# Softmax denominators of a graph-attention kernel: piece sums added by TensorE, or by VectorE after a block transpose

## The chip, the cores and the metric

The kernel runs on one core of a Trainium2 chip. The metric is the device time of one launch in microseconds (us). A core has TensorE (PE; its weight loads are shown as PEld), VectorE (DVE), ScalarE (ACT), GpSimd (POOL) and SyncE (SP). They run on their own queues, each in order, and wait for each other through semaphores. SP, ACT and POOL also issue the transfers (DMA).

## What is computed

There are N = 3327 nodes with 512 features and an adjacency matrix. Four layers follow each other, and each ends in `x = layernorm(x + layer(x))`. Layers 0, 2 and 3 are graph attention with 8, 8 and 4 heads; layer 1 averages over the first 64 neighbours. The attention layers have this core (layer 0, per head; the others differ in the width of a head and in an ELU at the end):

```python
Wh = jnp.einsum('ni,hio->hno', h, W)
e = jax.nn.leaky_relu(f1[:, :, None] + f2[:, None, :], ALPHA)
masked = jnp.where(adj[None] > 0, e, NEG_INF)
attention = jax.nn.softmax(masked, axis=-1)
h_prime = jnp.einsum('hnm,hmo->hno', attention, Wh)
```

A softmax row is a weighted sum of Wh divided by a denominator, the sum of its weights. The kernel computes numerators and denominators separately and divides later. This case is about the last step of the denominators.

## The kernel before

**Stages.** The kernel goes through layer 0's projection, layer 0's attention, layer 1 in two phases (`sage`), layer 2's attention, layer 3's projection (`third`), layer 3's attention and a tail. Nodes are cut into NT = 26 tiles of 128. The target nodes are cut into two halves of IW = 1664. In an attention layer `attention` (L516) runs over the two halves and over four units s of 128 feature columns. A unit holds HS heads: two in layers 0 and 2, one in layer 3.

**A unit** (`unit`, L357) loops over the 26 source tiles j. For each head, VectorE makes t, 128 source nodes by 1664 target nodes (L398), and ScalarE makes y from it, a step between the pieces of the weight (L401). TensorE multiplies t into the numerators, four PSUM tiles po0 to po3 (L421). Every second j, `den` multiplies y and the mask by narrow matrices of bf16 pieces into two PSUM tiles pd0 and pd1 (L373): these are the denominators. A bf16 piece holds a third of an fp32 number's digits. Every head has two numbers of three pieces each, in eight columns of these matrices, and each column's sums lie on a partition of their own in pd. Partitions 0 to 63 of pd hold the first WA = 896 target nodes, and 64 to 127 the other WB = 768. In layers 0 and 2 both heads have a group of 32 partitions; in layer 3 even and odd j have one each. The t tiles have three buffers a head, so VectorE runs at most three j ahead of TensorE. The tiles vj, the operand of numerators, come by SP two j at a time into four buffers (L409).

**After the loop.** po is copied to ob in SBUF (L441, L443) or transposed there by VectorE in 32x32 blocks (L439, layer 3's first half). `transposed` (L446) turns ob tile by tile on TensorE through two rotating PSUM banks, copies to hb (L453, two buffers) and stores to hd in DRAM (L454). When the last unit of a half is through (in layer 3's second half after units 1, 2 and 3), the pieces are added. ScalarE (in layer 3 VectorE for half of it) copies pd to db (L474, L475). `sums` (L479) lets TensorE multiply 13 tiles of db by a narrow matrix of 2, -2 and 0 (c1, or c1w for one head), which adds the pieces and at the same time turns target nodes onto partitions. `reciprocals` (L491) does two operations per head on VectorE and a reciprocal, and leaves the factors in rec. `finish_steps` (L165) later multiplies the h tiles by rec (L180), adds the residual and normalises (L152 to L161).

**What sets the order.** TensorE's order is the order in which the program is written (`manual_schedule`). The other engines' instructions are ordered by a planner with costs of its own, by when it thinks each ready; `keep_in_program_order` pins an instruction behind everything that was written before it for its engine. What follows a unit is put into a list of jobs, and the next unit's loop takes one job after each j: `jobs[:2] + [sums, nothing, reciprocals] + jobs[2:]` puts the sums after j = 2, the reciprocals after j = 4 and the first ob transposes after j = 5. After the second half of a layer no unit follows. The jobs are then run through one after the other, and the next stage's first tiles come behind them.

Of the kernel before, what the change touches and what calls it, by code (L numbers as in the profile page):

```python
# [7 lines left out]
F32 = mybir.dt.float32  # L8
# [5 lines left out]
ALU = mybir.AluOpType  # L14
AX = mybir.AxisListType
# [3 lines left out]
P = 128  # L19
# [13 lines left out]
def kernel(  # L33
# [10 lines left out]
    nc = tc.nc  # L44
# [5 lines left out]
    NS = F // P  # L50
    HALF = NT // 2
    FW = F // 2
    assert F == 512 and NT % 2 == 0 and N < NP and NT < 32
    IW = HALF * P
    NA = (HALF + 1) // 2
    WA, WB = NA * P, IW - NA * P
# [3 lines left out]
    QUADS = [(s, min(4, HALF - s)) for s in range(0, HALF, 4)]  # L60
# [5 lines left out]
    dram = ctx.enter_context(tc.tile_pool(name="dram", bufs=1, space=DRAM))  # L66
    qp = ctx.enter_context(tc.tile_pool(name="q", bufs=2, space=PSUM))
# [30 lines left out]
    c1 = const.tile([P, 2, 16], F32, name="c1")  # L98
    c1w = const.tile([P, 2, 2, 4], F32, name="c1w")
# [5 lines left out]
    for e in range(2):  # L105
        nc.vector.tensor_tensor(c1w[:, :, e, :], c1[:, :, 8 * e:8 * e + 4], c1[:, :, 8 * e + 4:8 * e + 8],
                                op=ALU.add)
# [4 lines left out]
    rec = const.tile([P, NT, 8], F32, name="rec")  # L112
# [110 lines left out]
    class Layer:  # L223
# [133 lines left out]
        def unit(self, pools, half, s, background, aside, final=None, ending=None):  # L357
            H, D, HS = self.H, self.D, self.HS
            tp, yp, vp, rp, sp, po_p = pools
# [3 lines left out]
            po = [po_p.tile([P, 512], F32, name=f"po{c}") for c in range(4)]  # L363
# [3 lines left out]
            pd, seen = self.pd, self.seen  # L367
# [76 lines left out]
            t0 = half * HALF  # L444

            def transposed(s0, n):  # L446
                pt = qp.tile([P, 4, P], F32, name="pt", tag="q")
                for q in range(n):
                    nc.tensor.transpose(pt[:, q, :], ob[:, (s0 + q) * P:(s0 + q + 1) * P], ident)  # L449
                if final:  # L450
                    return final(s, s0, n, pt)
                hb = sp.tile([P, 4, P], F32, name="hb")
                nc.scalar.copy(hb[:, :n], pt[:, :n])  # L453
                nc.sync.dma_start(out=hd[(t0 + s0) * P:(t0 + s0 + n) * P, s * P:(s + 1) * P]  # L454
                                  .rearrange("(t p) f -> p t f", p=P), in_=hb[:, :n])

            nothing = lambda: None
            jobs = [nothing, nothing]
            if by_dma:
                for b in range(4):  # L460
                    nc.sync.dma_start(out=hd[i0:i0 + IW, s * P + 32 * b:s * P + 32 * b + 32]
                                      .rearrange("(q i) f -> i q f", i=32),
                                      in_=ob[32 * b:32 * b + 32, :].rearrange("p (q f) -> p q f", f=32))
# [3 lines left out]
            if s < NS - 1 and not (final and s > 0):  # L467
                return jobs

            db = sp.tile([P, WA], F32, name="db", bufs=1)  # L470
            if WB < WA:
                nc.gpsimd.memset(db[64:, WB:], 0.0)
            for c in range(2):
                nc.scalar.copy(db[:64, c * (WA // 2):(c + 1) * (WA // 2)], pd[c][:64, :WA // 2])  # L474
                (nc.scalar.copy if HS == 2 else nc.vector.tensor_copy)(  # L475
                    db[64:, c * (WB // 2):(c + 1) * (WB // 2)], pd[c][64:, :WB // 2])
            held = []

            def sums():  # L479

                pe = po[0][:, :2 * HALF * H].rearrange("p (q o h) -> p q o h", q=HALF, o=2) if final and s == NS - 1 else \
                    qp.tile([P, HALF, 2, H], F32, name="pe", tag="q")
                held.append(pe)
                for q in range(HALF):
                    e = int(q >= NA)
                    cc = c1[:, :, 8 * e:8 * e + 8] if HS == 2 else c1w[:, :, e, :]
                    nc.tensor.matmul(pe[:, q, :, :], db[:, (q - e * NA) * P:(q - e * NA + 1) * P], cc,  # L487
                                     start=True, stop=True)


            def reciprocals():  # L491
                pe = held[0]

                ss = slice(0, NS) if not final else slice(0, 2) if s == 1 else slice(s, s + 1)
                r_ = rec[:, t0:t0 + HALF, :H].rearrange("p t (s k) -> p t k s", k=HS)
                rc = self.rc[:, t0:t0 + HALF, :].rearrange("p t (s k) -> p t k s", k=HS)
                pv = pe.rearrange("p t o (k s) -> p t o k s", k=HS)
                for k in range(HS):
                    tc.keep_in_program_order(
                        nc.vector.tensor_tensor(r_[:, :, k, ss], pv[:, :, 0, k, ss], rc[:, :, k, ss], op=ALU.mult))  # L500
                    nc.vector.tensor_tensor(r_[:, :, k, ss], pv[:, :, 1, k, ss], r_[:, :, k, ss], op=ALU.add)
                hs = slice(ss.start * HS, ss.stop * HS)
                nc.vector.reciprocal(rec[:, t0:t0 + HALF, hs], rec[:, t0:t0 + HALF, hs])

            if final and s == NS - 1:

                take = []
                return [lambda: take.append(transposed(*QUADS[0])), lambda: take.append(transposed(*QUADS[1])),
                        sums, reciprocals] + [lambda q=q: take[q]() for q in range(2)] + \
                    [lambda q=q: transposed(*q)() for q in QUADS[2:]]  # L510
            return jobs[:2] + [sums, nothing, reciprocals] + jobs[2:]

# [568 lines left out]
```

## Time and profile before

| | |
|---|---|
| median of 3 runs | 3428.16 us (3425.46 to 3432.74) |
| profiled execution | 3434.45 us, span 3432.3 us, mean granted TensorE clock 0.982 |
| layer 0, attention | to 960 us |
| layer 1 and the projection of layer 2 | 960 to 1790 us |
| layer 2, attention | 1790 to 2576 us |
| layer 3, projection, attention and tail | 2576 to 3432 us |
| sums on TensorE (L487) | at 580, 963, 2194, 2577, 3064, 3239, 3325 and 3403 us; 26 records each |
| copies of pd to db | L474 ACT 64x448: 0.52 us; L475 ACT 64x384: 0.47 us, DVE 64x384: 0.56 us |

The profile is one execution. A row of a group reads: line, engine, operation, output<-input with shapes and count, then busy time, mean ns of one, and the idle time of the engine just before, with what ended most of it. A row of a timeline reads: start, length, engine, line, operation, count, and in brackets an idle stretch before it and what ended it. A matmul of fp32 operands has two records; durations of pipelined matmuls overlap, so their rate is read from starts.

### The profile page before, as it was taken

The numbers are of one execution on the slowest core, as the hardware profiler recorded it, in microseconds if no ns is written. First come the engines' busy times: TensorE is split into PE (matmuls) and PEld (weight loads), VectorE is DVE, ScalarE is ACT, GpSimd is POOL, SyncE is SP. The second block draws the span as 40 slices with busy tenths as digits, with TensorE's granted clock in tenths as the row PEclk, the third lists the DMA queues.
The fourth block names the chain that finished last, engine by engine and source line by source line (L and its number), as shares of the span: only waits on it lengthen the run. The fifth ranks groups of instructions, "written<-read, shape, count | busy, mean of one in ns | idle before, by whom it ended". The sixth has DMA issues, their size and how long they took to land.

```text
span 3432.3 us, 47383 instructions
## 1 busy us (share of the span) xinstructions
PE 3295.2 (96%) x18705; PEld 1656.3 (48%) x18705; DVE 2666.0 (78%) x2571; ACT 2374.3 (69%) x2172; POOL 215.1 (6%) x344
## 2 busy tenths in 40 slices
PE   8799999999999899999989999999998999999997
PEld 7544344444444355555543444444446654455553
DVE  5799999999967443434349999999997766668876
ACT  2388999999943233333338999899997655559985
POOL 3200000000010111111110000000001000000000
PEclk9999999999999999999999999999998999999998
DMA  9732111111043422222220111111116411112211
GB/s 372 279 110 69 51 48 43 53 45 39 26 140 125 127 81 76 71 71 73 70 70 25 43 49 48 53 49 46 32 34 219 160 40 40 42 47 89 82 37 48
DMA packets 225061, 276.62 MB, mean 81 GB/s; under 512 B 45949, under 2 KB 160327, under 8 KB 224840
## 3 DMA queue, kind: packets, MB, share of 16 engines
q1 hardware_dynamic: 192280, 162.21, 14.8%
q0 software_dynamic: 27040, 103.70, 9.6%
q10 hardware_dynamic: 5520, 7.69, 0.7%
q8 instruction: 148, 2.42, 0.3%
q14 instruction: 73, 0.60, 0.1%
HBM read 204.92 MB, written 68.60 MB: 80 GB/s over the span
## 4 chain that ended last, share of the span: by engine, by line
PE 73%; issue 12%; DMA 6%; DVE 4%; ACT 3%; POOL 1%; SPq 0%; POOLq 0%; ACTq 0%; DVEq 0%
PE po L421 49%; PE pd L373 7%; PE acc L767 5%; DVE t L398 3%; PE pw L264 3%; PE pz L655 3%; PE pi L658 3%; DMA raw<-in_adjT_dram 2%; DMA cy<-ctd 2%; ACT y L401 1%; PE pt L449 1%; PE pe L487 1%; DMA r<-rr 0%; POOL cy L624 0%; PE pa L966 0%
## 5 line engine op out<-in xcount | busy, mean ns | idle before, releaser
L398 DVE SCALAR_TENSOR_TENSOR t<-rb,qc,mask 128x1664 f32<-128x1664 f32 x1040 | 1959.0, 1945 | 183.1 <-PE po L421 163.6
L401 ACT ACTIVATE y<-t,bi,sc 128x1664 fp8e4<-128x1664 f32 x1040 | 1770.0, 1766 | 321.7 <-PE pd L373 302.9
L421 PE MATMUL po<-t,vj 128*64 128x448 f32 (+3 forms) x8320 | 1912.8, 521 | 24.4 <-DVE t L398 24.2
L421 PEld LDWEIGHTS po<-t,vj 128*64 128x64 f32 (+1 forms) x8320 | 835.0, 148 | 978.1 <-issue 710.6
L767 PE MATMUL acc<-zs,kt 128*128 128x512 bf16 x1352 | 404.7, 381 | 0.0
L767 PEld LDWEIGHTS <-kt 128*128 128x128 fp8e4 x2028 | 199.3, 98 | 246.0 <-issue 9.6
L264 PE MATMUL pw<-wsb,xT 128*128 128x264 f32 (+1 forms) x1248 | 302.7, 398 | 9.6 <-DVE vt L270 5.1
L727 ACT CAST pk<-cy 128x512 f32<-128x512 bf16 x169 | 98.4, 587 | 287.1 <-DVE kt L739 234.0
L264 PEld LDWEIGHTS pw<-wsb,xT 128*128 128x128 f32 x1248 | 241.5, 197 | 55.9 <-ACT xT L255 6.0
L373 PE MATMUL pd<-y,sden 128*32 128x448 fp8e4 (+1 forms) x4160 | 259.4, 342 | 8.2 <-ACT y L401 8.2
L767 PE MATMUL acc<-zl,kt 128*128 128x512 bf16 x676 | 257.5, 381 | 4.6 <-DMA zl<-zd 4.6
L739 DVE SCALAR_TENSOR_TENSOR kt<-pk,mask 128x512 fp8e4<-128x512 f32 x169 | 116.2, 688 | 108.2 <-PE pk L735 107.8
L373 PEld LDWEIGHTS <-sden 128*32 128x32 bf16 x4160 | 117.5, 96 | 160.3 <-issue 137.6
L270 DVE TENSOR_TENSOR vt<-pw,dc 128x256 f32<-128x256 f32 x156 | 59.2, 416 | 136.7 <-ACT dc L265 129.7
L352 POOL DMA_DIRECT2D rb<-r x40 | 21.3, 533 | 1607.9 <-DVE t L398 1593.4
L268 ACT COPY rc<-pw 128x8 f32<-128x8 f32 (+1 forms) x78 | 12.7, 163 | 151.0 <-PE pw L264 151.0
L655 PE MATMUL pz<-wn,xT 128*128 128x512 f32 x208 | 93.7, 593 | 1.2 <-ACT xT L649 1.2
L658 PE MATMUL pi<-wl,xT 128*128 128x512 f32 x208 | 93.5, 592 | 0.0
L558 DVE TENSOR_SCALAR mask<-raw 128x832 fp8e4<-128x832 int32 (+2 forms) x95 | 56.2, 600 | 45.6 <-DMA raw<-in_adjT_dram 45.2
L747 DVE SCALAR_TENSOR_TENSOR y<-acc,cnt,bnb 128x512 f32<-128x512 f32 x26 | 19.5, 751 | 88.5 <-PE acc L767 88.5
L624 POOL DMA_DIRECT2D cy<-ctd x91 | 67.9, 746 | 289.5 <-ACT pk L727 264.8
L256 DVE TENSOR_REDUCE xsum<-xT 128x4 f32<-128x512 f32 x78 | 53.0, 681 | 39.7 <-ACT xT L255 39.3
(175 smaller groups left out, 1738.4 us busy)
## 6 DMA issues: line engine op xcount, KB each, us to landing
vj<-v SPq DMA_DIRECT2D x312, 128.0 KB
rb<-r POOLq DMA_DIRECT2D x40, 832.0 KB, 4.6
raw<-in_adjT_dram SPq DMA_DIRECT2D x67, 416.0 KB
cy<-ctd POOLq DMA_DIRECT2D x78, 256.0 KB, 3.9
h<-hd SPq DMA_DIRECT2D x61, 256.0 KB
v<-vt SPq DMA_DIRECT2D x50, 256.0 KB
hd<-hb SPq DMA_DIRECT2D x48, 256.0 KB
xr<-x POOLq DMA_DIRECT2D x45, 256.0 KB, 3.1
```

The costliest lines, as they stand in the source:

```text
L264: nc.tensor.matmul(pw[e][:, :FW + H], xT[:, c, :], wsb[:, c, e, :], start=c == 0, stop=c == FC - 1)
L270: nc.vector.tensor_tensor(vt[:, hs, :], pw[e][:, :FW].rearrange("p (h d) -> p h d", d=D), self.dc[:, t, hs].rearrange("p (h e) -> p h e", e=1)
L373: nc.tensor.matmul(pd[c][32 * kk:32 * kk + 32, :w_], lhsT, rhs, start=(kk, c) not in seen, skip_group_check=final is not None, stop=last a ...
L398: nc.vector.scalar_tensor_tensor(t, rb[k], self.qc[:, j, h:h + 1], mask[:, j, i0:i0 + IW], op0=ALU.max, op1=ALU.mult)
L401: nc.scalar.activation(y, t, AF.Sigmoid, bias=self.bi[:, j, h:h + 1], scale=self.sc[:, j, h:h + 1], saturate=False)
L421: nc.tensor.matmul(po[c][k * D:(k + 1) * D, :z - a_], vj[:, j % 2, k * D:(k + 1) * D], ts[k][:, a_:z], start=j == 0, stop=j == NT - 1)
L624: nc.gpsimd.dma_start(out=cy[:, :n, :], in_=ctd[t:t + n, b * GW:(b + 1) * GW] .rearrange("(o t) i -> o t i", o=1).to_broadcast([P, n, GW]))
L655: nc.tensor.matmul(pz, xT[:, c, :], wn[:, c, :], start=c == 0, stop=c == FC - 1)
L658: nc.tensor.matmul(pi, xT[:, c, :], wl[:, c, :], start=c == 0, stop=c == FC - 1)
L727: nc.scalar.copy(pks[k % 2], carry[b, t // 4 * 4][:, t % 4:t % 4 + 2, :])
L739: nc.vector.scalar_tensor_tensor(kt, pk, NEIGHBOURS, mask[:, t:t + 2, i0:i0 + GW], op0=ALU.is_le, op1=ALU.mult, saturate=False)
L767: nc.tensor.matmul(acc, kts[t][:, s * P:(s + 1) * P], zs(t, c) if c < 2 else zl[:, t, :], start=t == 0 and c == 0, stop=t == NT - 1 and c ...
```

## The change

For seven of the eight sums, all but that of layer 3's last unit, `sums` and `reciprocals` are replaced. VectorE transposes pd in 32x32 blocks into db straight out of PSUM, so a node's 32 piece columns lie side by side on its partition. Two reductions add three columns each into red. Four transfers on SP write red to a DRAM tile dd, in runs of 32 bytes, and a fifth loads it back as pes with the nodes on all 128 partitions; pes has red's buffer. `finish_sums` multiplies and adds as the old `reciprocals` did (in layer 3 with one addition before), with the factors 2 and -2 in its instructions, and takes the reciprocal. It comes after j = 6 in place of j = 4, and at the end of layers 0 and 2 after the ob transposes. The ob transposes begin after j = 2 (in unit 2 of layer 3's second half after j = 6). The PSUM tile pe, the 13 products and the copies of pd are gone there. The last unit's sum keeps its code.

```diff
+            if not (final and s == NS - 1):
+                for c in range(2):
+                    nc.vector.transpose(db[:64, c * (WA // 2):(c + 1) * (WA // 2)], pd[c][:64, :WA // 2])
+                    nc.vector.transpose(db[64:, c * (WB // 2):(c + 1) * (WB // 2)], pd[c][64:, :WB // 2])
+                red = sp.tile([P, WA // 32, 2, NS], F32, name="red", bufs=1)
+                dv = db.rearrange("p (b s x) -> p b s x", s=NS, x=8)
+                for o in range(2):
+                    nc.vector.tensor_reduce(red[:, :, o, :], dv[:, :, :, 3 * o:3 * o + 3], AX.X, ALU.add)
+                dd = dram.tile([IW, 2, 2 * NS], F32, name=f"dd{self.li}{half}{s}")
+                for kk in range(4):
+                    i_, w_ = (0, WA) if kk < 2 else (WA, WB)
+                    nc.sync.dma_start(out=dd[i_:i_ + w_, kk % 2, :].rearrange("(b i) x -> i b x", i=32),
+                                      in_=red[32 * kk:32 * kk + 32, :w_ // 32].rearrange("p b o s -> p b (o s)"))
+                pes = sp.tile([P, HALF, 2, 2, NS], F32, name="pes", tag="red", bufs=1)
+                nc.sync.dma_start(out=pes.rearrange("p q k o s -> p q (k o s)"),
+                                  in_=dd.rearrange("(q p) k x -> p q (k x)", p=P))
+                def finish_sums():
+                    if HS == 1:
+                        tc.keep_in_program_order(
+                            nc.vector.tensor_tensor(pes[:, :, 0], pes[:, :, 0], pes[:, :, 1], op=ALU.add))
+                    for k in range(HS):
+                        ins = nc.vector.scalar_tensor_tensor(r_[:, :, k, ss], pes[:, :, k, 0, ss], 2.0, rc[:, :, k, ss],
+                                                             op0=ALU.mult, op1=ALU.mult)
+                        if HS > 1:
+                            tc.keep_in_program_order(ins)
+                        nc.vector.scalar_tensor_tensor(r_[:, :, k, ss], pes[:, :, k, 1, ss], -2.0, r_[:, :, k, ss],
+                                                       op0=ALU.mult, op1=ALU.add)
+                    nc.vector.reciprocal(rec[:, t0:t0 + HALF, hs], rec[:, t0:t0 + HALF, hs])
+                jobs += [nothing] * max(0, 6 - len(jobs))
+                at = 6 if half == 0 or s < NS - 1 else len(jobs)
+                if final and s > 1:
+                    return [nothing] * 5 + [finish_sums] + jobs[2:]
+                return jobs[:at] + [finish_sums] + jobs[at:]
...
-                    cc = c1[:, :, 8 * e:8 * e + 8] if HS == 2 else c1w[:, :, e, :]
-                    nc.tensor.matmul(pe[:, q, :, :], db[:, (q - e * NA) * P:(q - e * NA + 1) * P], cc,
+                    nc.tensor.matmul(pe[:, q, :, :], db[:, (q - e * NA) * P:(q - e * NA + 1) * P], c1w[:, :, e, :],
...
-            return jobs[:2] + [sums, nothing, reciprocals] + jobs[2:]
```

More of the change, by code (lines that the diff above doesn't have):

```diff
@@ L468, in unit @@
                 return jobs
+            ss = slice(0, NS) if not final else slice(0, 2) if s == 1 else slice(s, s + 1)
+            hs = slice(ss.start * HS, ss.stop * HS)
+            r_ = rec[:, t0:t0 + HALF, :H].rearrange("p t (s k) -> p t k s", k=HS)
+            rc = self.rc[:, t0:t0 + HALF, :].rearrange("p t (s k) -> p t k s", k=HS)
             db = sp.tile([P, WA], F32, name="db", bufs=1)
@@ L473, in unit @@
             for c in range(2):
                 nc.scalar.copy(db[:64, c * (WA // 2):(c + 1) * (WA // 2)], pd[c][:64, :WA // 2])
-                (nc.scalar.copy if HS == 2 else nc.vector.tensor_copy)(
-                    db[64:, c * (WB // 2):(c + 1) * (WB // 2)], pd[c][64:, :WB // 2])
+                nc.vector.tensor_copy(db[64:, c * (WB // 2):(c + 1) * (WB // 2)], pd[c][64:, :WB // 2])
             held = []
             def sums():
-                pe = po[0][:, :2 * HALF * H].rearrange("p (q o h) -> p q o h", q=HALF, o=2) if final and s == NS - 1 else \
-                    qp.tile([P, HALF, 2, H], F32, name="pe", tag="q")
+                pe = po[0][:, :2 * HALF * H].rearrange("p (q o h) -> p q o h", q=HALF, o=2)
@@ L492, in reciprocals @@
                 pe = held[0]
[L494 to L502, printed above, removed]
-                nc.vector.reciprocal(rec[:, t0:t0 + HALF, hs], rec[:, t0:t0 + HALF, hs])
[L505 to L510, printed above, removed]
-            return jobs[:2] + [sums, nothing, reciprocals] + jobs[2:]
+                nc.vector.tensor_tensor(r_[:, :, 0, ss], pe[:, :, 0, ss], rc[:, :, 0, ss], op=ALU.mult)
+                nc.vector.tensor_tensor(r_[:, :, 0, ss], pe[:, :, 1, ss], r_[:, :, 0, ss], op=ALU.add)
+                nc.vector.reciprocal(rec[:, t0:t0 + HALF, hs], rec[:, t0:t0 + HALF, hs])
+            take = []
+            return [lambda: take.append(transposed(*QUADS[0])), lambda: take.append(transposed(*QUADS[1])),
+                    sums, reciprocals] + [lambda q=q: take[q]() for q in range(2)] + \
+                [lambda q=q: transposed(*q)() for q in QUADS[2:]]
         def attention(self, rp, extra=None, aside=(), later=None, final=None, ending=None):
```

## Prediction

> **What bounds the kernel now.** I read the page first, then tables of busy time by stage, then the waits of each stage, and last the timelines around the eight places where the sums are made. The page names two engines that could be the bound.
>
> ```profile
> PE 3295.2 (96%) x18705; PEld 1656.3 (48%) x18705; DVE 2666.0 (78%) x2571; ACT 2374.3 (69%) x2172; POOL 215.1 (6%) x344
> L398 DVE SCALAR_TENSOR_TENSOR t<-rb,qc,mask 128x1664 f32<-128x1664 f32 x1040 | 1959.0, 1945 | 183.1 <-PE po L421 163.6
> L421 PE MATMUL po<-t,vj 128*64 128x448 f32 (+3 forms) x8320 | 1912.8, 521 | 24.4 <-DVE t L398 24.2
> ```
>
> Which one it is depends on the stage. Here are one unit of layer 0 and the second half of layer 3 (columns: stretch, its length, then busy us of PE, PEld, DVE, ACT, POOL, granted clock, DMA share, GB/s), and the layer-3 waits:
>
> ```profile
> 766.47:863.33 96.86, 95.87 (x688) 40.51 (x689) 96.86 (x53) 90.19 (x60) 0.53 (x1) 1.00 0.12 36
> 3060.00:3403.00 343.00, 341.14 (x1467) 176.37 (x1465) 265.35 (x259) 283.39 (x223) 12.44 (x23) 1.00 0.19 58
> ```
>
> ```profile
> DVE t L398 <- PE po L421: 44.1, 43, 3.7
> PE pd L373 <- ACT y L401: 1.8, 1, 1.8
> ```
>
> In layers 0 and 2 (two heads a unit) VectorE is busy for the whole 96.86 us and waits for nothing; TensorE has about 1 us to spare. In layer 3 TensorE is busy 341 of 343 us, VectorE waits 44.1 us for it. So **the same trade, TensorE time for VectorE time, should lose in layers 0 and 2 and win in layer 3.** A layer-3 place on TensorE (start, length):
>
> ```profile
> 3055.32 8.65 PE L421 MATMUL po<-t,vj 128*128 128x448 f32 x24
> 3063.80 2.96 PE L487 MATMUL pe<-c1w,db 128*128 128x8 f32 x26
> 3066.62 4.74 PE L421 MATMUL po<-t,vj 128*128 128x448 f32 x8
> ```
>
> No wait stands on either side: the sums take 3066.62 - 3063.80 = 2.82 us of the bound. The 4.74 us after them is 3.04 us at the other two layer-3 places (from 3242.17 and 3327.55); the granted clock is 0.70 to 0.73 here.
>
> The ends of layers 0 and 2 are different: the sums have nothing beside them. The end of layer 0 over all engines:
>
> ```profile
> 965.48 4.45 PE L487 MATMUL pe<-c,db 128*128 128x16 f32 x20 [1.72 <-ACT db L475]
> 969.96 0.21 DVE L500 TENSOR_TENSOR rec<-pe,rc 128x52 f32<-128x52 f32 x1 [7.62 <-PE pe L487]
> 978.40 0.69 DVE L180 TENSOR_TENSOR h<-h,rec 128x512 f32<-128x512 f32 x1 [4.09 <-DMA h<-hd]
> 984.85 0.33 PE L647 MATMUL pt<-ident,h 128*128 128x128 f32 x1 [1.84 <-ACT h L161]
> ```
>
> PE starts sums at 962.91, ob's transposes at 969.55 (ob was complete at 957.80), and the first wide product at 975.87. From 984.85 to 1165 PE is busy without a gap, so what 984.85 moves by is kept. At the end of layer 2 the chain goes through ScalarE and VectorE:
>
> ```profile
> 2583.42 0.59 ACT L453 COPY hb<-pt 128x512 f32<-128x512 f32 x1 [3.99 <-PE pt L449]
> 2589.27 0.17 DVE L155 RECIPROCAL rs<-rs 128x2 f32<-128x2 f32 x1 [2.72 <-ACT rs L154]
> 2592.09 1.97 PE L253 MATMUL pt<-ident,h 128*128 128x128 f32 x8 [3.93 <-ACT h L161]
> ```
>
> **What the Trainium skill says.** (1) "VectorE: DVE Perf Modes", section "The three transpose paths": VectorE transposes only separate 32x32 blocks. That is why the block's eight piece columns land along the free axis, where a reduction can add them. The trace has this operation out of PSUM already (L439, 0.574 us median, against 0.621 us for a plain copy of 128x448 at L443), which agrees with a transpose costing what a copy costs. (2) "DMA: Bandwidth & Descriptors", section "Anatomy of one DMA": a transfer has about 2.0 us of fixed cost, and a wait for a semaphore is spent on the issuing queue before dispatch. The trace agrees on an idle moment (xr loads land in 3.0 us) and not on a full one: h loads at the end of layer 0 land in 9.0 us. (3) "TensorE: Matmul & The Clock Gate", section "What's actually happening": the clock is halved after a free-running window in which the array had little to do, so whether a short slack stretch is caught depends on the phase. In the trace the clock fell after two of the five sums that lie inside loops (at 2196 and 3064) and nowhere else inside them, so I count part of that to the sums.
>
> **The change part by part.** Seven of eight sums change; the last keeps its form.
>
> Removed on PE: 13 products, 26 records a place. Layer 3, three places (3063.80, 3239.35, 3324.73): 2.82 us each, **-8.5 us**. The clock loss after the first is 4.74 - 3.04 = 1.7 us; bounds 0 and -1.7, I take **-0.9**.
>
> Added on DVE: four block transposes at 0.525 us pitch (four at 3053.70 take 2.10) = 2.1 us; two reductions of 336 elements. From L101 (48 elements, 0.202 us) and L256 (512, 0.681) the slope is 1.03 ns, so 0.50 us each. Together 3.1 us. The multiply-adds stay four of 0.2 us for two heads. In layer 3 two copies of 0.557 us go and one add of about 0.25 comes, so +2.3 us net, which lies in VectorE's 44 us of waits; a burst can hold one t back: 0 to +1, I take **+0.5** for all three.
>
> First halves of layers 0 and 2: PE's 3 us and ACT's four copies (2 us) go, but neither is the bound. VectorE's 3.1 us is, with no cover, less what it waited for PE at that place: 0.44 us (577.58) and 1.39 us (2203.32). So +2.6 and +1.7: **+4.3** (bounds +3 to +6, the upper one if a transpose stands in the queue ahead of its last denominator product). The transposes of ob move three slots forward there; PE does the same work.
>
> The new transfers: four writes and one load on SP, 3,328 runs of 32 bytes and 1,664 of 64. L461's 6,656 runs of 128 bytes kept the DMA engines full for 6.2 us (3057 to 3063.3), 0.93 us a thousand, so about 3.1 and 1.5 us (bounds half and twice: no row has runs this short). With landing at idle prices a round trip is about 9 us, under load up to 2 x 9 = 18. The load waits on SP for the writes; behind it stand vj loads, which run three pairs ahead (22 us of cover in layer 0, 17 in layer 3), and at the layer ends hb stores and h loads. On DVE the finishing arithmetic is pinned behind what was traced before it, slot 6; t runs about three slots ahead, so VectorE gets there some 18.6 us after the boundary (L503 now comes 17.7 after it): cover for a trip of about 15.5 us after 3.1 us of VectorE work. I take 0 there. POOL's memset of db waits for a reduction in place of the products; behind it stand rb loads with slack of a unit.
>
> End of layer 0: PE can transpose ob from about 961, 8.5 us sooner; with hb's two buffers and their stores of 2.9 us, the first wide product comes about 6 sooner. But 984.85 needs tiles 2 and 3, whose loads land at about 971 and 972 in either kernel; DVE then needs six steps of 0.68 us, and statistics and scaling take until about 977. That bounds the gain at 8. It is 0 if the finish stands ahead of those steps and its transfers take 18 us. I take **-5.5**.
>
> End of layer 2: ACT loses 2 us of copies, its hb copies come some 6 us sooner, so L154 is bound by VectorE's statistics (2583.84 now, about 1 us later with the new work): L155 could come 2.7 us sooner. If the finish is queued ahead of it, it comes at 2591 instead. Bounds -4 and +3; I take **-1.0**.
>
> Sum: -8.5 - 0.9 + 0.5 + 4.3 - 5.5 - 1.0 = **-11.1 us**. The profiled execution took 3434.45 us (span 3432.3 and 2.15 around it), 6.3 above the median of 3428.16; against it the sum gives 3423.3, and against the median, which I forecast, **3417.1**. About 0.2%, 6.9 us, is what a measurement of this kernel tells from no change.
>
> **Rivals.** *Only layer 3 pays:* the two ends give nothing, because VectorE and SP wait for the round trip where VectorE waited for PE. For it speak 9.0 us landings; against it that DVE waits 7.62 us there already. -8.5 - 0.9 + 0.5 + 4.3 = -4.6: 3423.6. *Slower:* each of the two transfers takes 9 us at four places in layers 0 and 2, and VectorE stands behind the finish: end of layer 2 +9.5 (red done at 2579.2, 18 us, 1.6 of finish, against 2589.27), end of layer 0 +0.6, first halves 18 - 15.5 = 2.5 each. -4.6 + 9.5 + 0.6 + 5.0 = +10.5: 3438.7. It decides from a round trip of about 17 us; the first halves' light traffic (DMA share 0.14) speaks against it. That the change doesn't do what it says would show in L487's records; it is plainly in the code.
>
> **How the numbers follow.** Forecast 0.57, only layer 3 pays 0.27, slower 0.16. The forecast's own bounds are -19 to -7. Faster: 0.50 of the forecast and 0.06 of the second case, 0.56; slower 0.15 of the third; same 0.29. The range 3409 to 3433 takes in the first two and the near part of the third.
>
> **What would show it.** Right: L487 falls from 208 to 26 records; each layer-3 unit after a boundary is 2.8 us shorter; VectorE's share in the first unit of the second half in layers 0 and 2 grows by 3 us and that unit by 2 to 3; L647's tile 2 comes some 5 us sooner after the last den product. Wrong: a wait of DVE for DMA pes of more than 3 us in a loop, a new PE wait for DVE t in layer 3, or L155 later at layer 2's end.

## The result, and the profile after

In runs beside each other on one chip the changed kernel takes 3427.78 us (median of 4 runs) and the kernel before 3429.25 us (4 runs): ratio 0.9995, 95% interval 0.9977 to 1.0012. With more runs (21 and 41) it is 3429.28 against 3433.87 us, ratio 0.9986, interval 0.9980 to 0.9993. So it is faster by about 4.6 us (2.4 to 6.9), where 11.1 us had been forecast. That is 0.13%, less than the 0.2% named in the prediction; only the many runs tell it from nothing. The sign is right and the size is not: 4.6 lies outside the forecast's own bounds of 7 to 19 us.

The profiled execution took 3425.27 us (span 3423.6; before 3434.45 and 3432.3). The busy times of the page:

```profile
PE 3274.8 (96%) x18523; PEld 1638.8 (48%) x18523; DVE 2684.0 (78%) x2610; ACT 2361.0 (69%) x2148; POOL 215.1 (6%) x344
L398 DVE SCALAR_TENSOR_TENSOR t<-rb,qc,mask 128x1664 f32<-128x1664 f32 x1040 | 1958.8, 1944 | 168.0 <-PE po L421 150.9
L421 PE MATMUL po<-t,vj 128*64 128x448 f32 (+3 forms) x8320 | 1921.5, 520 | 26.8 <-DVE t L398 21.3
```

TensorE lost 20.4 us of work and 182 instructions (7 times 26), VectorE gained 18 us. The trade is as described. What it did to the time is read stage by stage. A stage ends here where the last denominator product (L373) of a unit ends, as everything about the sums comes after it:

| stage (us) | before | after | difference | forecast |
|---|---|---|---|---|
| start to end of layer 0's first half | 571.75 | 569.28 | -2.5 | 0 |
| layer 0, second half, first unit | 97.87 | 100.76 | +2.9 | +2.6 |
| end of layer 0 to layer 2's first unit | 933.99 | 936.48 | +2.5 | -5.5 |
| layer 2, second half, first unit | 99.66 | 101.36 | +1.7 | +1.7 |
| end of layer 2 to layer 3's first unit | 235.97 | 233.08 | -2.9 | -1.0 |
| layer 3, second half, units 0, 2 and 3 | 261.53 | 251.40 | -10.1 | -8.9 |
| tail | 30.60 | 30.16 | -0.4 | 0 |

The first row ends before the changed code is reached, so its 2.5 us are scatter of the first stages, and a part of what these two profiles differ by. The rows that are left out, the units without a boundary, differ by 0.1 us or less.

**Layer 3.** A unit of layer 0 without a boundary (the third of its second half), then layer 3's second half from end to end, and two waits of the latter:

```profile
766.89:863.75 96.86, 95.87 (x687) 40.54 (x689) 96.86 (x53) 90.21 (x60) 0.53 (x1) 1.00 0.12 36
3057.20:3393.40 336.20, 334.42 (x1393) 168.63 (x1393) 275.46 (x277) 281.65 (x217) 12.44 (x23) 1.00 0.23 63
```

```profile
DVE t L398 <- PE po L421: 32.4, 35, 1.9
PE pd L373 <- ACT y L401: 1.8, 1, 1.8
```

The kernel before has the same second half at 3055.39 to 3401.70:

```profile
3055.39:3401.70 346.31, 344.53 (x1470) 177.88 (x1471) 269.07 (x261) 286.72 (x225) 12.44 (x23) 1.00 0.20 60
```

VectorE has 6.4 us more to do (269.07 to 275.46), close to the three times 2.3 of the prediction, and its waits for TensorE fell from 44.1 to 32.4 us: the work went into the waits. TensorE is still the bound, and at the boundary its timeline has no hole left where the products stood:

```profile
3056.27 0.94 PE L373 MATMUL pd<-y,sden 128*32 128x448 fp8e4 x16
3057.13 11.44 PE L421 MATMUL po<-t,vj 128*128 128x448 f32 x32
```

**The end of layer 0**, by engine (TensorE, ScalarE, VectorE, SP); the last denominator product ends at 961.37. L449 turns ob, L686 is the first wide product, pz, and L678 turns tile 2 of layer 1 (L647 before):

```profile
961.30 1.09 PE L449 MATMUL pt<-ident,ob 128*128 128x128 f32 x8
...
975.39 6.11 PE L686 MATMUL pz<-wn,xT 128*128 128x512 f32 x8 [9.13 <-ACT xT L680]
...
988.15 1.11 PE L678 MATMUL pt<-ident,h 128*128 128x128 f32 x4 [3.22 <-ACT h L161]
```

```profile
974.03 0.82 ACT L453 COPY hb<-pt 128x512 f32<-128x512 f32 x2 [8.47 <-DMA hd<-hb]
```

```profile
979.63 0.21 DVE L503 SCALAR_TENSOR_TENSOR rec<-pes,rc 128x52 f32<-128x52 f32 x1 [14.77 <-DMA pes<-dd]
```

```profile
962.88 1.30 SPq L454 DMA_DIRECT2D hd<-hb  x2
964.89 9.64 SPq L491 DMA_DIRECT2D dd<-red  x4
974.64 1.03 SPq L454 DMA_DIRECT2D hd<-hb  x2
977.04 0.36 SPq L494 DMA_DIRECT2D pes<-dd  x1
977.50 2.23 SPq L126 DMA_DIRECT2D h<-hd  x4
```

The same place before, TensorE, ScalarE and SP (the last product ends at 960.94):

```profile
969.76 3.41 PE L449 MATMUL pt<-ident,ob 128*128 128x128 f32 x13
974.42 0.90 ACT L453 COPY hb<-pt 128x512 f32<-128x512 f32 x2 [1.78 <-DMA hd<-hb]
971.50 3.89 SPq L454 DMA_DIRECT2D hd<-hb  x3
975.45 0.51 SPq L126 DMA_DIRECT2D h<-hd  x1
```

TensorE turns ob 8.5 us sooner than before (961.30 for 969.76), but pz stays at 14.0 us after the last denominator product (before 14.9), and tile 2 comes 26.8 us after it in place of 23.9. Between them: two stores of hb leave at 962.88 and hb is free only at 974.03 (before 971.50 and 974.42); four small writes take 9.64 us to be issued on SP; VectorE stands 14.77 us for the last of the five transfers.

**The end of layer 2** (ScalarE, then VectorE; last denominator product at 2580.41):

```profile
2582.92 1.05 ACT L453 COPY hb<-pt 128x512 f32<-128x512 f32 x2
2590.78 0.99 ACT L453 COPY hb<-pt 128x512 f32<-128x512 f32 x2 [6.81 <-DMA hd<-hb]
```

```profile
2593.42 0.17 DVE L155 RECIPROCAL rs<-rs 128x2 f32<-128x2 f32 x1 [2.80 <-ACT rs L154]
```

L155 comes 13.0 us after the last product, 13.6 before. The finish of the sums doesn't stand ahead of it; it runs at 2597.31. A store stands in the way of the 2.7 us that the prediction named here too: hb's first copy comes 5.2 us sooner, but the third waits 6.81 us for a store that left at 2583.51, and L154, which L155 needs, stands behind it on ScalarE.

### The profile page after: what moved, and what is told of

Same layout as the page of the kernel before. It is cut to its first block, busy times and chain, and to the rows that moved or that the text cites. A ratio compares the mean times of both kernels' runs of the same rounds, so it can differ in the third digit from the quotient of the medians.

```text
span 3423.6 us, 47127 instructions
## 1 busy us (share of the span) xinstructions
PE 3274.8 (96%) x18523; PEld 1638.8 (48%) x18523; DVE 2684.0 (78%) x2610; ACT 2361.0 (69%) x2148; POOL 215.1 (6%) x344
## 3 DMA queue, kind: packets, MB, share of 16 engines
q1 hardware_dynamic: 227784, 163.71, 15.4%
## 4 chain that ended last, share of the span: by engine, by line
PE 74%; issue 10%; DMA 7%; DVE 6%; ACT 2%; POOL 1%; SPq 0%; ACTq 0%; POOLq 0%; DVEq 0%
PE po L421 49%; PE pd L373 7%; PE acc L798 7%; PE pw L264 4%; DVE t L398 4%; PE pz L686 3%; PE pi L689 3%; DMA cy<-ctd 2%; DMA raw<-in_adjT_dram 2%; ACT y L401 1%; PE pt L449 1%; DMA h<-hd 1%; PE pt L253 1%; PE pk L766 0%; PE pa L997 0%
## 5 line engine op out<-in xcount | busy, mean ns | idle before, releaser
L421 PE MATMUL po<-t,vj 128*64 128x448 f32 (+3 forms) x8320 | 1921.5, 520 | 26.8 <-DVE t L398 21.3
L421 PEld LDWEIGHTS po<-t,vj 128*64 128x64 f32 (+1 forms) x8320 | 844.5, 148 | 980.9 <-issue 698.9
L264 PE MATMUL pw<-wsb,xT 128*128 128x264 f32 (+1 forms) x1248 | 300.6, 396 | 12.6 <-DVE vt L270 10.9
L373 PE MATMUL pd<-y,sden 128*32 128x448 fp8e4 (+1 forms) x4160 | 259.4, 342 | 8.2 <-ACT y L401 8.2
L373 PEld LDWEIGHTS <-sden 128*32 128x32 bf16 x4160 | 117.6, 96 | 160.2 <-issue 137.6
L686 PE MATMUL pz<-wn,xT 128*128 128x512 f32 x208 | 98.5, 618 | 9.1 <-ACT xT L680 9.1
```

What stands on the lines that cost most here:

```text
L264: nc.tensor.matmul(pw[e][:, :FW + H], xT[:, c, :], wsb[:, c, e, :], start=c == 0, stop=c == FC - 1)
L373: nc.tensor.matmul(pd[c][32 * kk:32 * kk + 32, :w_], lhsT, rhs, start=(kk, c) not in seen, skip_group_check=final is not None, stop=last a ...
L421: nc.tensor.matmul(po[c][k * D:(k + 1) * D, :z - a_], vj[:, j % 2, k * D:(k + 1) * D], ts[k][:, a_:z], start=j == 0, stop=j == NT - 1)
L686: nc.tensor.matmul(pz, xT[:, c, :], wn[:, c, :], start=c == 0, stop=c == FC - 1)
```

## The experiments

The theory after the first result: the terms add up as forecast except the one for the end of layer 0, where the wait for the sums was replaced by waits on transfers that fall among that moment's loads (the weights wn and wl of 1 MB each, blb, h and xr on POOL's queue). Rivals: the loss at that place is VectorE's wait for pes alone; or SP's queue, which the small writes hold, alone; or the terms don't add and layer 3 paid less than forecast. All medians stand beside the kernel before on the same chip:

| run | us (runs) | before | ratio, 95% interval |
|---|---|---|---|
| e1_again | 3429.28 (21) | 3433.87 | 0.9986 (0.9980 to 0.9993) |
| e2_l3 | 3422.69 (5) | 3433.87 | 0.9964 (0.9951 to 0.9976) |
| e3_halves | 3436.77 (13) | 3433.87 | 1.0006 (0.9998 to 1.0014) |
| e4_ends | 3437.36 (13) | 3433.87 | 1.0008 (1.0000 to 1.0016) |
| e5_late | 3442.39 (13) | 3433.40 | 1.0027 (1.0018 to 1.0035) |
| e6_wl | 3427.29 (21) | 3433.40 | 0.9985 (0.9978 to 0.9991) |
| e7_red2 | 3427.88 (11) | 3433.40 | 0.9984 (0.9975 to 0.9993) |
| e8_mix | 3418.46 (5) | 3433.40 | 0.9950 (0.9936 to 0.9964) |
| e9_none | 3424.94 (9) | 3433.06 | 0.9976 (0.9966 to 0.9986) |
| e10_nowait | 3427.29 (20) | 3433.06 | 0.9985 (0.9978 to 0.9991) |
| e11_pool | 3428.41 (20) | 3433.06 | 0.9989 (0.9981 to 0.9997) |
| e12_order | 3420.29 (8) | 3433.06 | 0.9967 (0.9956 to 0.9978) |

### The change in three parts: e1_again, e2_l3, e3_halves, e4_ends

e1 is the changed kernel once more. The others take the new way at some places only and the old code at the rest (the lines that bring it back are left out):

```diff
-            if not (final and s == NS - 1):
+            if not (final and s == NS - 1) and HS == 1:            # e2: layer 3
+            if HS == 2 and half == 0:                              # e3: first halves of layers 0 and 2
+            if HS == 2 and half == 1:                              # e4: ends of layers 0 and 2
```

> The changed kernel once more, beside the others. Theory (the change is a sum of terms by place: layer 3 about -10 us, first halves of layers 0 and 2 about +4.6, end of layer 0 about +2.7, end of layer 2 about -2.5): about 5 us faster than before. Rival (nothing moves but the profile's own scatter): within 1 us of before.

> The new way in layer 3 alone (three places); layers 0 and 2 as before. Theory: the 13 products are taken off an engine that is busy without a gap, 3 x 2.8 = 8.5 us, and 1.8 more where the granted clock falls after the first: 8 to 10 us faster than before. Rival (VectorE's bursts or the transfers hold layer 3 up as well): 0 to 3 us faster.

> The new way at the first halves of layers 0 and 2 alone. Theory (VectorE is the bound there, so its 3.4 us more are paid, less the 0.4 and 1.4 us it waited for TensorE): the first unit of the second half grows by 2.9 us in layer 0 and by 1.7 in layer 2, the kernel by about 4.6. Rival (TensorE bounds these units as the chain of waits has it, and gains 3 us each): 3 to 6 us faster.

> The new way at the ends of layers 0 and 2 alone. Theory (the round trip and the stores wait for full DMA engines, so that what TensorE saves comes to nothing): end of layer 0 about 3 us later, end of layer 2 up to 3 us sooner, the kernel within 3 us of before. Rival (my forecast's sum): 6.5 us faster. VectorE waits 10 us or more for pes at the end of layer 0 by the theory, under 5 by the rival.

Measured against the kernel before: -4.6 us for the whole, -11.2 for layer 3, +2.9 for the first halves, +3.5 for the ends. The three parts add to -4.8, the whole is -4.6: **the terms add, as near as these medians tell (the interval of e3 goes from -0.7 to +4.8 us, that of e4 from 0.0 to +5.5), and layer 3 did pay.** What is missing of the forecast was lost at the ends of layers, by the stage table at that of layer 0: there e4's tile 2 comes 27.5 us after the last denominator product, and VectorE waits 15.44 us for pes. Over all profiled kernels, tile 2 comes 22.6 to 24.2 us after it with the old code at this place (before, e2, e3, e8) and 26.6 to 27.5 with the new (after, e1, e4, e7). The stage from there to layer 2's first unit is 908.6 to 912.3 us longer than that time in all 14 kernels, so what tile 2 moves by is kept.

### What one microsecond of VectorE costs: e7_red2

```diff
                 for o in range(2):
                     nc.vector.tensor_reduce(red[:, :, o, :], dv[:, :, :, 3 * o:3 * o + 3], AX.X, ALU.add)
+                for o in range(2):
+                    nc.vector.tensor_reduce(red[:, :, o, :], dv[:, :, :, 3 * o:3 * o + 3], AX.X, ALU.add)
```

> The changed kernel with the two reductions done twice at each of the seven places, 1.0 us more of VectorE each time. Theory (VectorE is the bound in layers 0 and 2 and has slack in layer 3): the first unit of the second half grows from 100.8 to 101.8 us in layer 0 and from 101.4 to 102.4 in layer 2; layer 3's units after a sum stay at 86.2, 82.6 and 82.7; the kernel is about 2 us slower than the changed one. Rival (TensorE bounds both): no unit grows.

The first boundary of layer 0 on VectorE:

```profile
572.35 0.98 DVE L487 TENSOR_REDUCE red<-db 128x112 f32<-128x336 f32 x2
573.24 0.96 DVE L489 TENSOR_REDUCE red<-db 128x112 f32<-128x336 f32 x2
574.11 5.68 DVE L398 SCALAR_TENSOR_TENSOR t<-rb,qc,mask 128x1664 f32<-128x1664 f32 x3
```

The second pair takes 574.11 - 573.24 = 0.87 us. The first unit of the second half grows by 0.88 us in layer 0 (100.76 to 101.64) and by 0.90 in layer 2 (101.36 to 102.26). In layer 3 unit 0 has 86.33 us for 86.16 and unit 3 exactly the same 82.67; unit 2 has 84.27, as in e1, with a drop of the clock that comes back below. So in layers 0 and 2 each microsecond of VectorE at a boundary is a microsecond of its unit, and in layer 3 almost none is. The whole kernel isn't slower (3427.88 us): 1.8 us in two units is below its scatter.

### The end of layer 0, first tries: e5_late, e6_wl

e5 puts the last finish of layer 0 behind the finishing steps of tiles 4 to 7 of layer 1; e6 issues the loads of wl and blb behind those of tiles 2 and 3.

```diff
+                if self.li == 0 and half == 1:          # e5
+                    self.put_off = finish_sums
+                    return jobs
...
+                    if t0 == 4:
+                        prev.put_off()
```

```diff
-                wl = load_w(wp, wlT, "wl", nc.gpsimd)   # e6
+                wl = wp.tile([P, FC, F], F32, name="wl")
...
-                nc.gpsimd.dma_start(out=blb, in_=bl.to_broadcast([P, F]))
...
+                    if t0 == 0:
+                        nc.gpsimd.dma_start(out=wl, in_=wlT.rearrange("(c p) m -> p c m", p=P))
+                        nc.gpsimd.dma_start(out=blb, in_=bl.to_broadcast([P, F]))
```

> The changed kernel, with layer 0's last finishing arithmetic issued later, behind the finishing steps of tiles 4 to 7 of the next stage, so that VectorE no longer stands before its transfers. Theory A (two things hold the end of layer 0: VectorE's 15 us wait, and hb stores that land late because the DMA engines are full, so that the first wide product starts at 14 to 15 us after the last denominator product in either way): tile 2's transposes move from 27 us after it back to about 24, as before the change, and the kernel gains about 3 us on the changed one. Rival B (VectorE's wait alone): tile 2 comes at about 19, and the kernel gains 7 or 8 on the changed one.

> The changed kernel, with two loads of layer 1 (wl, 1 MB, and blb) issued behind the loads of tiles 2 and 3 and no longer ahead of them. Theory A (the DMA engines are full at the end of layer 0, and hb's stores and the round trip wait for that): the first wide product moves from 14.4 us after the last denominator product to 11 or less, the wait for pes from 15 us to 10 or less, tile 2's transposes from 27 to 22 or less. Rival (the round trip is that long by its own short runs and issue): all three stay within 1.5 us.

Neither gave what was expected. In e5 VectorE no longer waits for pes, but 8.75 us for an h load that SP issues behind the small writes, and the planner put ScalarE's copies of xT behind the normalisation of tiles 2 to 5: pz at 33.1 us, tile 2 at 42.0, and 9.0 us slower than before. In e6 the wait for pes is gone too (0.46 us) and a 9.56 us wait for the same kind of load stands there; pz at 20.3, tile 2 at 28.8. Taking one wait away let the next show itself, at about the same time. Both also changed the planner's order, so neither says what the sums by themselves cost at this place. The next four do.

### The end of layer 0 settled: e9_none, e10_nowait, e11_pool

e9 leaves the sums of layer 0's second half out; e10 keeps all their work and transfers but doesn't use the loaded pes; e11 issues the five transfers on POOL.

```diff
+            if self.li == 0 and half == 1:                            # e9
+                def plain():
+                    for k in range(HS):
+                        ins = nc.vector.tensor_copy(r_[:, :, k, ss], rc[:, :, k, ss])
+                        tc.keep_in_program_order(ins)
+                    nc.vector.reciprocal(rec[:, t0:t0 + HALF, hs], rec[:, t0:t0 + HALF, hs])
+                return jobs + [plain]
```

```diff
                 def finish_sums():
+                    if self.li == 0 and half == 1:                    # e10
+                        for k in range(HS):
+                            ins = nc.vector.tensor_copy(r_[:, :, k, ss], rc[:, :, k, ss])
+                            tc.keep_in_program_order(ins)
+                        nc.vector.reciprocal(rec[:, t0:t0 + HALF, hs], rec[:, t0:t0 + HALF, hs])
+                        return
```

```diff
+                eng = nc.gpsimd if self.li == 0 and half == 1 else nc.sync      # e11
...
-                    nc.sync.dma_start(out=dd[i_:i_ + w_, kk % 2, :].rearrange("(b i) x -> i b x", i=32),
+                    eng.dma_start(out=dd[i_:i_ + w_, kk % 2, :].rearrange("(b i) x -> i b x", i=32),
...
-                nc.sync.dma_start(out=pes.rearrange("p q k o s -> p q (k o s)"),
+                eng.dma_start(out=pes.rearrange("p q k o s -> p q (k o s)"),
```

> The changed kernel, but at the end of layer 0 the sums are left out wholly: no block transposes, no reductions, no transfers, and rec there is the reciprocal of rc alone, so the denominators of layer 0's second half are left out. It bounds what any way of making these sums can give at this place. Theory (the products were only partly on the path: the first wide product waits for hb's stores to land among the full loads, and tile 2 for its h load): pz 11 to 14 us after the last denominator product, tile 2 at 17 to 21 us (23.9 in the kernel before, 26.8 in the changed one), and the time 5 to 9 us below the changed kernel's. Rival (the step of the prediction: the sums were fully on the path, and their end gives 5.5 us or more against the kernel before): tile 2 at 15 to 18 us.

> The changed kernel, with the transposes, the reductions and the five transfers kept at the end of layer 0, but VectorE doesn't use pes there: rec is the reciprocal of rc alone, so the denominators of layer 0's second half are left out. VectorE has no wait for the round trip; SP has all of its transfers. Theory (SP's queue, held by the four writes, keeps hb's later stores and the h loads back, and is a cause by itself): pz about 14 us after the last denominator product, tile 2 at 23 to 27 us, and VectorE waits for DMA h<-hd in place of pes. Rival (VectorE's wait for pes alone makes the loss): tile 2 at 18 to 21 us.

> The changed kernel with the five transfers of the end of layer 0 issued on POOL's queue in place of SP's; nothing is left out. Theory (SP's blocked queue is a holder of its own beside the round trip): hb's stores and the h loads of tiles 4 and 5 are issued within 3 us of SP's turn, pes still takes 10 us or more, and tile 2 comes 1 to 5 us sooner than the changed kernel's 26.8 us. Rival (the round trip alone decides): tile 2 within 1 us of 26.8.

| end of layer 0 (us) | before | after | e9_none | e10_nowait | e11_pool |
|---|---|---|---|---|---|
| last denominator product to pz | 14.9 | 14.0 | 14.1 | 14.2 | 5.9 |
| to tile 2 | 23.9 | 26.8 | 24.6 | 26.8 | 30.1 |
| to layer 2's first unit | 933.99 | 936.48 | 934.71 | 936.36 | 940.12 |

**e9 decides, and neither side had expected it** (tile 2 at 17 to 21, or 15 to 18): with no sums at all tile 2 comes at 24.6 us, no sooner than with TensorE's products (22.6 to 24.2). Its ScalarE, its VectorE and its SP show why (last denominator product at 960.79):

```profile
973.40 0.91 ACT L453 COPY hb<-pt 128x512 f32<-128x512 f32 x2 [9.18 <-DMA hd<-hb]
```

```profile
978.58 1.29 DVE L180 TENSOR_TENSOR h<-h,rec 128x512 f32<-128x512 f32 x2 [6.79 <-DMA h<-hd]
```

```profile
962.30 12.62 SPq L454 DMA_DIRECT2D hd<-hb  x4
975.01 1.83 SPq L126 DMA_DIRECT2D h<-hd  x4
```

The first stores leave at 962.30 and hb is free at 973.40, 11.1 us later; hb's third copy waits for that, SP waits for the third copy, and the h loads stand behind it on SP. They leave at 975.01, 14.2 us after the last product. Before, the stores left 9 us later, counted from the last product, and took 2.9, and the h loads left at 975.45, 14.5 us after it. VectorE's 4.09 us wait for h at 978.40, which the prediction shows, was the mark of this second chain: products and loads went side by side, and the loads ended last. This bounds the gain for the order that the kernel has, with ScalarE's copies of xT behind hb's third copy and SP's loads behind the stores; a third buffer for hb, or the h loads ahead of the stores, was not run.

e10 gives tile 2 at 26.8 us as the changed kernel does, though VectorE never waits for pes. It waits for the loads instead, 9.04 us, because SP's queue is late by itself (VectorE, then SP):

```profile
980.41 1.29 DVE L180 TENSOR_TENSOR h<-h,rec 128x512 f32<-128x512 f32 x2 [9.04 <-DMA h<-hd]
963.79 9.90 SPq L491 DMA_DIRECT2D dd<-red  x4
973.79 1.16 SPq L454 DMA_DIRECT2D hd<-hb  x2
976.34 0.36 SPq L494 DMA_DIRECT2D pes<-dd  x1
976.80 2.70 SPq L126 DMA_DIRECT2D h<-hd  x4
```

The h loads leave 16.5 us after the last product (976.80 - 960.26), 2.3 later than in e9; tile 2 is 2.2 us later. So the wait for pes alone doesn't make the loss; SP's queue is enough for all of it. It is not the only holder, as e11 shows on POOL and on VectorE:

```profile
965.77 2.94 POOL L492 DMA_DIRECT2D dd<-red  x4 [7.28 <-DVE red L487]
968.69 0.77 POOL L137 DMA_DIRECT2D wl<-in_wlT_dram  x1
974.89 1.15 POOL L495 DMA_DIRECT2D pes<-dd  x1 [5.43 <-DMA dd<-red]
```

```profile
979.94 0.21 DVE L504 SCALAR_TENSOR_TENSOR rec<-pes,rc 128x52 f32<-128x52 f32 x1 [14.47 <-DMA pes<-dd]
```

SP is free: hb is free again 2.9 us after the stores leave, SP's h loads leave at 968.05, and pz stands at 5.9 us in place of 14. But VectorE still waits 14.47 us for pes, now wl comes late (pi waits 5.16 us for it), and the h loads of tiles 2 and 3, which POOL issues, stand behind pes. Tile 2 comes 3.3 us later than in the changed kernel. Its expectation of 1 to 5 us sooner is wrong; the round trip is a holder too, of about the same length: it lets VectorE go on 18.0 us after the last product, the h loads of e10 20.2 us after it.

### Other mixtures: e8_mix, e12_order

e8 takes the new way in layer 3 and at the end of layer 2, and the old one in layer 0 and in layer 2's first half. e12 is e8 with TensorE's products at the end of layer 0 behind the first two groups of ob's transposes.

```diff
-            if not (final and s == NS - 1):
+            if not (final and s == NS - 1) and (HS == 1 or self.li == 2 and half == 1):    # e8
...
+                if self.li == 0 and half == 1:                                             # e12
+                    return jobs[:6] + [sums, nothing, reciprocals] + jobs[6:]
```

> The new way in layer 3 and at the end of layer 2; the rest as before. Theory (terms add; the end of layer 2 gives 1 to 3 us): 12 to 14 us faster than before. Rival (the end of layer 2 gives nothing, what the profiles differ by there is the planner's order of the next stage): 9 to 11 us faster, as with layer 3 alone.

> The best kernel so far (the new way in layer 3 and at the end of layer 2 only), with TensorE's products at the end of layer 0 written behind the first two groups of ob's transposes in place of ahead of them; nothing is left out. Theory (early transposes gain little, since their stores wait among the full loads, and products in that gap cost little): pz 12 to 15 us, tile 2 at 22 to 25 us after the last denominator product, the time within 3 us of the best one's. Rival (the products ahead of the transposes are what holds the start of layer 1): tile 2 at 16 to 20 us and 4 us or more faster.

e8 has the lowest median of the study, 14.9 us below the kernel before, where the changed kernel is 4.6 below it; it is a little more than the 12 to 14 expected. By the intervals e8 is told apart from the changed kernel, but not from e2 or e12. e12 is 12.8 us below the kernel before. Its stores leave at 963.80, and hb is free at 973.15:

```profile
973.15 0.93 ACT L453 COPY hb<-pt 128x512 f32<-128x512 f32 x2 [8.88 <-DMA hd<-hb]
```

pz comes at 15.9 us, tile 2 at 27.3, later than expected and far from the 16 to 20 us of the rival. Transposes that start sooner gain nothing here, as in e9.

## Why the prediction was right in sign and wrong in size, point by point

- **Layer 3's products, -8.5: right.** Units 0, 2 and 3 are shorter by 4.60, 2.81 and 2.71 us; without the 1.71 us of slow clock in the first this is 2.89 + 2.81 + 2.71 = 8.4.
- **Its clock, -0.9: right in kind, too small.** Three profiled kernels have the old sums there (before, e3, e4). Right after them they lost 1.71, 3.41 and 3.42 us to the clock, 2.8 on average. That is more than the term's bound of 1.7; e2's -11.2 agrees with -8.4 - 2.8, though its interval (-16.8 to -8.2) doesn't prove it.
- **Held-back t's, +0.5: nothing.** TensorE's waits for t are 21.3 us in the whole kernel, 24.2 before.
- **First halves, +4.3: right, one of the two by accident.** +2.9 and +1.7 by the profiles. VectorE's additions take 2.53 us of its queue for the four transposes (569.13 to 571.66; the term had 2.1) and 0.90 for the two reductions (573.53 to 574.43; the term had 1.0), 3.43 in all; less the 0.44 us of wait that is 3.0 in layer 0, where 2.9 were measured. But layer 2's first unit took 99.66 us before only because the clock was at half for 6.8 us; with the old code it takes 97.95 at a full clock (e4, e8, e12) and 98.02 with half as long a drop (e2), so that the price is +3.4, the whole of VectorE's additions. The 1.39 us for which VectorE waited there was the slow clock, and no cover.
- **The finish inside loops, 0: right.** Of the changed kernel's finishes only the one at the end of layer 0 waits for pes, and in no run is such a wait inside a loop longer than 1.88 us (e12). At the first boundary the writes are issued in 2.08 us and the load of pes at 578.36; VectorE uses it at 591.19.
- **The end of layer 0, -5.5: this step failed.** It measures +2.5 us of stage and +2.9 at tile 2. The step said that "with hb's two buffers and their stores of 2.9 us, the first wide product comes about 6 sooner". The 2.9 us were read at 971.5 to 974.4 us, when most of the loads were through. Moved 8.6 us ahead, the stores fall among the loads and take 11.1 us. And tile 2 was said to need loads that "land at about 971 and 972 in either kernel"; but in VectorE's queue the work on an h load of SP's, at 978.40, stood ahead of tile 3's statistics, which are normalised together with tile 2's, and that load stands behind the stores. e9 shows that nothing was to be gained in this order; e10 and e11 show how the new way lost 2.5 us on top. The rival "only layer 3 pays" gave 3423.6 by the same cause, a wait of VectorE and SP in place of one for TensorE, and its change of -4.6 is what was measured. That the number fits is in part luck: it has nothing at either end and 0.9 for the clock, where the profiles have +2.5, -2.9 and 2.8. Of the signs named for being right, tile 2's failed, and layer 2's unit grew by 1.7 us in place of 2 to 3; of those for being wrong, none came.
- **The end of layer 2, -1.0: within its bounds, not settled.** -2.9 us in the profiled kernel, of which L155 shows 0.6, and e8 is 3.7 us below e2 by the medians' differences. But the stage that follows takes 235.97, 240.21 and 237.15 us in three kernels with the old code at its head, and 230.2 to 239.0 (middle one 233.0) in eleven with the new: the planner's order in that stage differs, and moves as much as the term.

With the measured terms the sum is -8.4 - 2.8 + 2.9 + 3.4 + 2.5 - 2.9 = -5.3 us, inside the interval of the whole. The rival with 18 us round trips needed them at four places; 14.5 to 15.4 us of wait were measured at one (after, e1, e4, e11), and there SP's queue alone holds tile 2 as long (e10).

## What to carry to other kernels

A duration of a transfer belongs to the moment at which it was read. When an edit moves a store or a load by several microseconds, ask what else the DMA engines carry at the new time; here 2.9 us became 11.1, and the 8 us that TensorE had saved were gone. Before pricing the removal of a wait, look for the second chain that ends at the same instruction (here VectorE's 4.09 us for h): a run that leaves the step out wholly tells what it can be worth at most. And the same trade between two engines may be taken place by place: where TensorE was the bound it gave 11 us, where VectorE was it cost about 3 us a place, and the mixture beat both kernels.

## What the runs showed of the hardware that was not expected

**A store beside loads.** The first store of hb, 256 KB, took 11.1 to 11.7 us until its buffer was free in the seven kernels whose wl load had been issued 1.8 us ahead of it (after, e1, e4, e5, e7, e9, e10), 9.4 where it was 5.4 us ahead (e12), 7.7 where wl came 0.5 us after it, with other loads ahead (e6), and 2.3 to 3.6 where wl was 10.9 us ahead (before, e2, e3, e8) or 5.2 us behind (e11). The packets of the changed kernel show two parts of it. Of each queue they give the packets, MB and share of the DMA engines; q0 has POOL's loads, q1 SP's transfers. From 962.88 to 967.50, then from 968 to 971 us:

```profile
q0 software_dynamic: 355, 1.34, 93.9%
```

```profile
q0 software_dynamic: 309, 1.03, 84.6%
q1 hardware_dynamic: 330, 0.17, 18.6%
```

In the first 4.6 us no packet of the store moves. Then both queues move about as many packets (296 and 327 in e9, 283 and 294 in e10), but SP's have about 0.5 KB each and POOL's 3.3, so the store gets 0.17 MB of 1.20. This agrees with the Trainium skill's "DMA: Bandwidth & Descriptors", section "Queues, rings and completion order", by which a DMA engine takes turns between queues packet by packet: turns are not equal shares of bytes. Why SP's queue has no turn in the first 4.6 us is left open.

**Issuing can be what is slow.** The same four writes of 3,328 runs of 32 bytes took SP 2.08 us at the first boundary, where no other queue moved anything, 2.2 to 4.5 at the end of layer 2 and 8.9 to 10.3 at the end of layer 0, and everything behind them on SP waited. The DMA share alone doesn't set it: in the changed kernel it is 1.07 during the 4.18 us of layer 2 and 0.91 during the 9.64 of layer 0.

**The clock after narrow products.** Of the 19 old sums inside loops in the profiled kernels, 8 were followed by a granted clock of about one half for 3.4 or 6.8 us, from 1.1 us before their end to 1.1 us after it; of the 51 places with the new way, none. One of them, in the kernel before, ahead of it, during it and after it (granted clock is third from last):

```profile
2192.50:2196.00 3.50, 3.50 (x29) 2.49 (x25) 3.50 (x3) 3.50 (x3) 0.00 (x0) 1.00 0.12 36
2196.00:2203.00 7.00, 7.00 (x26) 3.08 (x25) 5.94 (x7) 3.89 (x3) 0.20 (x1) 0.53 0.00 0
2203.00:2210.00 7.00, 7.00 (x64) 3.29 (x64) 6.54 (x5) 5.43 (x4) 0.00 (x0) 0.99 0.07 21
```

TensorE shows as busy in all three; the granted clock of the second is 0.53. Over the 19 sums the clock took 17.1 us of TensorE's time, 0.9 us a sum, about a third of what the products themselves take. In layer 3, where TensorE is the bound, its 8.5 us lengthen the units by about as much; in layers 0 and 2, where VectorE is, 3.8 of 8.5 us showed in the units.

Which sums are caught is a matter of phase. The changes of the clock in a trace all stand on one grid of 3.413 us. The 8 sums that were followed by a drop cover 2.27 us or more of one interval of their grid, and the other 11 cover 2.22 or less. This agrees with "TensorE: Matmul & The Clock Gate", section "What's actually happening", as the prediction read it: windows catch a stretch of narrow products by their phase. So a profile in which no drop follows is no proof that the products are harmless. Other drops have no part in this: one in the first 4 us of layer 3's unit 2, in seven kernels with either way, and those at the head of layers 0 and 2 (before at 168.9, 1790.2 and 1807.3 us, inside loops too, which the prediction's "nowhere else inside them" passed over), where TensorE stands waiting between products.
